# Scatter-adds of one expert declared independent, and the zero fill of the expert rows moved to the kernel's start

## The chip, the cores and the metric

The program runs on one core of a Trainium2 chip. The metric is the device time of one execution in microseconds (us). Before the change it takes 4751.77 us, the median of three runs between 4748.73 and 4754.36 us. All profile times below count from the start of the profiled execution, whose span is 4751.6 us.

A core has five engines that run their own instruction streams in order: PE (TensorE, matrix products and transposes), DVE (VectorE), ACT (ScalarE), POOL (GpSimd) and SP (SyncE, here only a DMA queue). SP and ACT issue the plain transfers; POOL issues the indirect ones (scatters by a list of row numbers) and, in this kernel, the zero fills of large DRAM tables. An instruction that waits for a semaphore holds up everything behind it on its own engine, DMA issues included.

## The reference, cut to what matters

A graph of 3125 nodes with 256 features goes through four blocks, each added to its input:

- three attention layers over 103125 edges (a projection of the nodes, then edge scores, a softmax over the incoming edges and a weighted sum),
- a mixture of 16 experts, of which each node uses its best two,
- a layer that sums neighbours' messages,
- a mixture of 8 experts with one expert per node.

The change is in the second block and in what prepares it. Cut to that:

```python
logits = x @ gate_w + gate_b
top_probs, top_idx = top_k(softmax(logits), 2)
top_probs = top_probs / sum(top_probs)
hidden = silu(x @ w1[e]) * (x @ w2[e])           # for each expert e
out = sum over the two chosen e of weight[e] * (hidden @ w3[e])
```

Every node thus adds two rows, from two different experts, to its sum. Within one expert no node occurs twice.

## The kernel before, in words

**Tiling.** The nodes lie in 25 tiles of 128 rows (NT, NP = 3200 rows in all). The rows of each expert lie in a table in DRAM, `rows0`, with room for 3200 rows per expert, of which the first 512 (CAP0, four tiles of 128) are used. A row has 258 numbers (1032 bytes): 256 features, the node's number, and its weight. Places of an expert that no node takes must hold zero features and a node number that points to a spare row beyond the real nodes; this is why the first 512 rows of each expert are filled with an "empty" row (L579 to L585) before nodes are scattered into them.

**Routing (L593 to L661).** Layer norm, gate scores, softmax, the best two experts and each node's place in their tables are worked out on PE, DVE and ACT. The last result is `to`, the row numbers (L648). Then 50 indirect DMAs on POOL (L659), two for each tile of nodes, write the nodes' rows into `rows0`. They are declared independent of each other, but they come behind the zero fill, as they write the same table.

**Experts (L664 to L706).** A Python loop, unrolled, over the 16 experts. For expert e:

- ACT issues the loads of `w1`, `w2`, `w3` (L671 to L675), SP the load of the expert's rows `xs` (L677). Pools `rw` and `rx` have two buffers for each name, so what expert e+2 loads goes where expert e's was.
- DVE turns the node numbers of the rows into integers, `who` (L679). This name too has two buffers: `who` of expert e+2 overwrites that of expert e, and may do so only when expert e's scatters, which read it, are over.
- PE transposes the rows (L684), ACT copies them out (`xsT`, L685).
- For each of four slices j of the hidden width, PE forms `p1` and `p2` (both `ps_h` in the profile, L692; two PSUM buffers each), ACT applies silu to `p1` (L695), DVE multiplies by `p2` into `hid` (L696).
- For each of the four row tiles q, PE forms `ps_o` (L700), DVE scales it to `y` (L703), and POOL adds it to the nodes' rows of a DRAM table `sums` by an indirect DMA that accumulates (L704).

The four scatter-adds of an expert, and those of successive experts, all write `sums`, and the framework orders writers of one tensor: each waits for the landing of the one before. At the end `sums` is read back into `x` (L708).

In the profile each float32 product shows as two instructions: 32 of `ps_h` (four slices, two products, two halves of the inner dimension, times two) and 32 of `ps_o` for one expert.

**Order of the work.** The order on each engine comes from the framework's scheduler, not from the Python order alone: it lets later work pass when earlier work is not ready. In the trace DVE runs `who` of expert e+1 before `hid` of expert e.

**The start.** `setup` loads x; `routed` (L868) opens a pool `em` for one 5128-byte-per-partition tile and has POOL write it into the table of the last block, `rows1`, in nine DMAs (`empty_rows`, L854, 8 of 5128 KB and one of 641 KB). The pool closes, and `attention_layers` opens its own pools in the freed SBUF space: first `gw`, with, for each layer, `gw0` (2048 bytes per partition, issued by SP, L272), `ga0` (2048, ACT, L274 and L275) and `gb0` (1024, ACT, L277), then the same for the two other layers. A tile in reused space waits until the old tile's readers, here the zero-fill DMAs, have landed. The projection of the first layer follows (L222 on PE, copies L223 on ACT, scores L230 on DVE), then `build_adjacency`: a preparation (L80 to L135), which loads edges on SP and ACT, and a loop over groups of edges with bounds known only at run time (L157). Every turn of that loop ends with a meeting of all five engines.

Of the kernel before, what the change touches and what calls it, by code (L numbers as in the profile page):

```python
# [9 lines left out]
F32 = mybir.dt.float32  # L10
# [4 lines left out]
OP = mybir.AluOpType  # L15
# [4 lines left out]
P = 128  # L20
# [3 lines left out]
NP = NT * P  # L24
D = 256
# [9 lines left out]
NX0, HID0 = 16, 512  # L35
# [482 lines left out]
CAP0 = 512  # L518
CAP1 = 1024
SLOTS = (N + NX1 * (P - 1)) // P  # L520
ROW0 = D + 2
ROW1 = HID1 + D + 2
SPARE = NP


def counters(tc, cp):

    nc = tc.nc
    before = cp.tile([P, P], BF16, name="before")
    nc.gpsimd.memset(before, 1.0)  # L530

    nc.gpsimd.affine_select(before, before, pattern=[[1, P]], compare_op=OP.is_gt, fill=0.0, base=0,
                            channel_multiplier=-1)
    every = cp.tile([P, P], BF16, name="every")
    nc.gpsimd.memset(every, 1.0)
    return before, every


def independent(tc, group, made):

    tc.declare_no_dep(made.ins, group=group, reason="rows of different tokens")
    tc.add_to_no_dep_group(group, made.ins)
# [21 lines left out]
            nc.scalar.copy(xnT[:, :, t * P:(t + 1) * P], ps)  # L564


def routed_experts(tc, x, ident, eps, iota, count, gate_w, gate_b, w1, w2, w3, over):

# [2 lines left out]
    nc = tc.nc  # L573
    before, every = count
    nh = HID0 // P
    with tc.tile_pool(name="rd", bufs=1, space=DRAM) as dp, tc.tile_pool(name="r1", bufs=1) as cp:
        rows = dp.tile([NX0 * NP, ROW0], F32, name="rows0")
        sums = dp.tile([NP + P, D], F32, name="sums0")
        empty = cp.tile([P, ROW0], F32, name="empty")  # L579
        nc.vector.memset(empty, 0.0)  # L580
        nc.gpsimd.iota(empty[:, D:D + 1], pattern=[[0, 1]], base=SPARE, channel_multiplier=1,
                       allow_small_or_imprecise_dtypes=True)
        for e in range(NX0):
            nc.sync.dma_start(rows[e * NP:e * NP + CAP0].rearrange("(q p) f -> p q f", p=P),
                              empty[:, None, :].to_broadcast([P, CAP0 // P, ROW0]))  # L585
        nc.scalar.dma_start(sums[:NP].rearrange("(t p) f -> p t f", p=P), x)
        nc.scalar.dma_start(sums[NP:], empty[:, :D])
        gw = cp.tile([P, KD, NX0], F32, name="gate_w")
        nc.sync.dma_start(gw, gate_w.rearrange("(k p) e -> p k e", p=P))
        gb = cp.tile([P, NX0], F32, name="gate_b")  # L590
# [2 lines left out]
        with tc.tile_pool(name="rgk", bufs=1) as kp, tc.tile_pool(name="rgw", bufs=2) as wp, \  # L593
# [20 lines left out]
            for j, m in enumerate((m1, m2)):  # L614
# [6 lines left out]
                                    channel_multiplier=-1)  # L621
# [6 lines left out]
            for t in range(NT):  # L628
# [10 lines left out]
                           allow_small_or_imprecise_dtypes=True)  # L639
# [3 lines left out]
            for j, hot in enumerate((hot1, hot2)):  # L643
# [7 lines left out]
                           allow_small_or_imprecise_dtypes=True)  # L651
            for t in range(NT):
                n = P if t < NT - 1 else LAST
                for j in range(2):
# [6 lines left out]
                        in_=row[:n], in_offset=None, bounds_check=NX0 * NP - 1, oob_is_err=False))  # L661

        nq = CAP0 // P
        with tc.tile_pool(name="rw", bufs=2) as ep, tc.tile_pool(name="rx", bufs=2) as xp, \  # L664
             tc.tile_pool(name="rs", bufs=3) as sp, \
             tc.tile_pool(name="rpt", bufs=2, space=PSUM) as tp, \
             tc.tile_pool(name="rp1", bufs=2, space=PSUM) as pp, \
             tc.tile_pool(name="rp2", bufs=2, space=PSUM) as po:
            for e in range(NX0):
                a = ep.tile([P, KD, HID0], F32, name="w1")  # L670
                nc.scalar.dma_start(a, w1[e].rearrange("(k p) h -> p k h", p=P))  # L671
                b = ep.tile([P, KD, HID0], F32, name="w2")
                nc.scalar.dma_start(b, w2[e].rearrange("(k p) h -> p k h", p=P))
                o = ep.tile([P, nh, D], F32, name="w3")
                nc.scalar.dma_start(o, w3[e].rearrange("(k p) f -> p k f", p=P))  # L675
                xs = xp.tile([P, nq, ROW0], F32, name="xs")
                nc.sync.dma_start(xs, rows[e * NP:e * NP + CAP0].rearrange("(q p) f -> p q f", p=P))  # L677
                who = xp.tile([P, nq], I32, name="who")
                nc.vector.tensor_copy(who, xs[:, :, D])  # L679
                xsT = xp.tile([P, KD, CAP0], F32, name="xsT")  # L680
                for k in range(KD):
                    ps = tp.tile([P, CAP0], F32, name="ps_x")
                    for q in range(nq):
                        nc.tensor.transpose(ps[:, q * P:(q + 1) * P], xs[:, q, k * P:(k + 1) * P], ident)  # L684
                    nc.scalar.copy(xsT[:, k], ps)  # L685
                hid = xp.tile([P, nh, CAP0], F32, name="hid")
                for j in range(nh):
                    p1 = pp.tile([P, CAP0], F32, name="ps_h1")
                    p2 = pp.tile([P, CAP0], F32, name="ps_h2")
                    for ps, w in ((p1, a), (p2, b)):  # L690
                        for k in range(KD):
                            nc.tensor.matmul(ps, w[:, k, j * P:(j + 1) * P], xsT[:, k], start=(k == 0),  # L692
                                             stop=(k == KD - 1))
                    s = sp.tile([P, CAP0], F32, name="silu")
                    nc.scalar.activation(s, p1, AF.Silu)  # L695
                    nc.vector.tensor_tensor(hid[:, j], s, p2, op=OP.mult)  # L696
                for q in range(nq):
                    ps = po.tile([P, D], F32, name="ps_o")
                    for j in range(nh):
                        nc.tensor.matmul(ps, hid[:, j, q * P:(q + 1) * P], o[:, j], start=(j == 0),  # L700
                                         stop=(j == nh - 1))
                    y = sp.tile([P, D], F32, name="y")
                    nc.vector.tensor_scalar(y, ps, xs[:, q, D + 1:D + 2], None, op0=OP.mult)  # L703
                    nc.gpsimd.indirect_dma_start(  # L704
                        out=sums[:, :], out_offset=bass.IndirectOffsetOnAxis(ap=who[:, q:q + 1], axis=0),
                        in_=y, in_offset=None, bounds_check=NP + P - 1, oob_is_err=True, compute_op=OP.add)  # L706
            for t in range(0, NT, 5):
                nc.sync.dma_start(x[:, t:t + 5], sums[t * P:(t + 5) * P].rearrange("(t p) f -> p t f", p=P))  # L708

# [144 lines left out]
def empty_rows(tc, cp, rows):  # L854

    nc = tc.nc
    empty = cp.tile([P, ROW1], F32, name="empty1")
    nc.vector.memset(empty, 0.0)
    nc.gpsimd.iota(empty[:, HID1 + D:HID1 + D + 1], pattern=[[0, 1]], base=SPARE, channel_multiplier=1,
                   allow_small_or_imprecise_dtypes=True)  # L860
    for e in range(NX1):
        nc.gpsimd.dma_start(rows[e * NP:e * NP + CAP1].rearrange("(q p) f -> p q f", p=P),
                            empty[:, None, :].to_broadcast([P, CAP1 // P, ROW1]))
    nc.gpsimd.dma_start(rows[NX1 * NP:], empty)


@with_exitstack
def routed(ctx: ExitStack, tc: tile.TileContext, i: dict, out: bass.AP, over):  # L868
    nc = tc.nc
    const = ctx.enter_context(tc.tile_pool(name="const", bufs=1))  # L870
    dram = ctx.enter_context(tc.tile_pool(name="dram", bufs=1, space=DRAM))
    x, ident, eps, iota = setup(tc, const, i)
    count = counters(tc, const)
    rows = dram.tile([NX1 * NP + P, ROW1], F32, name="rows1")
    with tc.tile_pool(name="em", bufs=1) as em:
        empty_rows(tc, em, rows)

    ct = [dram.tile([P, NP], F32, name=f"ct{b}") for b in range(NT)]
    neg = [dram.tile([P, NP], BF16, name=f"neg{b}") for b in range(NT)]
    layers = [[i[f"L0_gnn_{n}{j}"] for n in ("W", "al", "ar", "b")] for j in (1, 2, 3)]  # L880
    attention_layers(tc, x, ident, eps, ct, neg, i["src"], i["dst"], layers)

    late = ctx.enter_context(tc.tile_pool(name="late", bufs=1))
    weights = top1_weights(tc, late, *(i["L1_ffn_" + n] for n in ("W1", "b1", "Wg", "bg", "Wd", "bd")), ident)
    routed_experts(tc, x, ident, eps, iota, count,
                   *(i["L0_ffn_" + n] for n in ("gate_w", "gate_b", "w1", "w2", "w3")), over[:, 0:1])
    xnT = late.tile([P, KD, NP], F32, name="xnT")
    layernorm_t(tc, x, xnT, ident, eps)
    sum_layer(tc, x, xnT, ct, i["L1_gnn_W"], i["L1_gnn_M"])
    layernorm_t(tc, x, xnT, ident, eps)  # L890
    routed_top1(tc, x, xnT, ident, iota[:, NX0 - NX1:], count, weights, rows, out, over[:, 1:2])
# [81 lines left out]
```

## Time and profile before

| What | Value |
|---|---|
| Device time | 4751.77 us |
| PE busy | 3457.9 us, 73% of the span |
| DVE busy | 2261.3 us, 48% |
| ACT busy | 769.3 us, 16% |
| POOL busy | 247.0 us, 5% |
| First projection product (L222) | at 122.69 us |
| First group of the edge loop (L161) | at 173.51 us |
| First indirect store of rows (L659) | at 3437.33 us |
| First expert's first product (L692) | at 3514.74 us |
| Last scatter-add landed, x read back from | 4004.88 us |

The span falls into the start and adjacency (to 1961 us), three attention layers (to about 3369 us), routing (to 3507 us), the 16 experts (to 4005 us), the sum layer and the last block. Only the chain view and the waits of one stage tell what that stage is bound by; the shares of the whole span are means over all of them.

### The profile page before, as it was taken

The page shows a single profiled execution, that of the slowest core. Times are in us where ns is not written, and L with a number is a line of the kernel's source. Part 1 is how long each engine was busy: PE and PEld are TensorE (multiplying, and loading weights), DVE is VectorE, ACT ScalarE, POOL GpSimd, SP SyncE. Part 2 cuts the span into 40 slices and gives each one's busy share as a digit, 9 for nine tenths or more (in the row PEclk, how much of TensorE's full clock was granted, in tenths as well). Part 3 has the DMA queues.
Part 4 walks back from the last instruction along what each step waited for, and adds up shares of the span by engine and source line. Part 5 has one row for each costly group of instructions (what it writes and reads, how often), then busy time and mean ns, then how long its engine had stood idle before and what let it go on. Part 6 is the DMA issues. An engine that isn't in the chain of part 4 may idle for free. (4 is left out here: it accounts for less than half of the span.)

```text
span 4751.6 us, 53978 instructions
## 1 busy us (share of the span) xinstructions
PE 3457.9 (73%) x15718; PEld 2262.2 (48%) x15718; DVE 2261.3 (48%) x5414; ACT 769.3 (16%) x822; POOL 247.0 (5%) x258
## 2 busy tenths in 40 slices
PE   0666666666666666588888888888537786998978
PEld 0322222222222222377767776777424443886456
DVE  1555555555555555576756665777411112002322
ACT  0100000000000000133333333333121111001310
POOL 0000000000000000000000000000042211000211
PEclk7788888888888898899999998999768887999989
DMA  9101000010010101233333333433633333331233
GB/s 386 27 35 42 28 35 32 31 42 28 35 42 21 42 28 42 106 137 129 142 118 132 138 132 119 152 145 139 200 114 81 89 88 106 111 139 56 109 121 111
DMA packets 122345, 452.30 MB, mean 95 GB/s; under 512 B 13778, under 2 KB 66834, under 8 KB 106133
## 3 DMA queue, kind: packets, MB, share of 16 engines
q1 hardware_dynamic: 57336, 260.79, 15.4%
q10 hardware_dynamic: 38478, 112.15, 6.8%
q0 software_dynamic: 26320, 76.75, 5.1%
q8 instruction: 106, 1.74, 0.1%
q14 instruction: 105, 0.86, 0.1%
HBM read 299.62 MB, written 151.02 MB: 95 GB/s over the span
## 5 line engine op out<-in xcount | busy, mean ns | idle before, releaser
L171 PE MATMUL acc<-ohk,ohs 125*128 125x512 f16 (+1 forms) x4260 | 1025.0, 393 | 497.1 <-DVE ohs L167 451.2
L339 PE MATMUL acc<-h,pt 128*128 128x257 f32 x3750 | 931.0, 398 | 160.4 <-DVE pt L335 160.3
L171 PEld LDWEIGHTS <-ohs 125*128 125x128 f16 x4260 | 423.0, 111 | 1102.5 <-DVE ohs L167 519.5
L339 PEld LDWEIGHTS acc<-h,pt 128*128 128x128 f32 x3750 | 715.2, 197 | 300.5 <-DVE pt L335 191.6
L169 DVE TENSOR_SCALAR ohk<-iota_k,kw 125x1600 f16<-125x1600 f16 x1065 | 672.1, 631 | 0.0
L335 DVE TENSOR_TENSOR pt<-ps_t,cb 128x512 f32<-128x512 f32 (+1 forms) x525 | 314.1, 626 | 406.2 <-PE ps_t L333 405.1
L167 DVE TENSOR_SCALAR ohs<-iota_s,sw 125x128 f16<-125x128 f16 x1065 | 249.4, 251 | 236.4 <-PE acc L171 234.7
L180 ACT COPY blk<-acc 128x512 f32<-128x512 f32 x98 | 57.4, 586 | 1740.6 <-PE acc L174 1702.1
L692 PE MATMUL ps_h<-xsT,w 128*128 128x512 f32 x512 | 259.9, 667 | 93.8 <-DVE hid L696 90.3
L325 ACT ACTIVATE z<-z,er 128x3200 f32<-128x3200 f32 x75 | 222.2, 2963 | 623.4 <-DVE r L343 589.0
L333 PE MATMUL ps_t<-ident,z 128*128 128x128 f32 x1875 | 243.6, 274 | 55.7 <-ACT z L327 55.7
L443 PE MATMUL ps_s<-msg,s_ct 128*128 128x256 f32 x1250 | 273.9, 379 | 0.0
L319 DVE CUSTOM_DVE_ANT_0 z<-el_row,nb 128x3200 f32<-128x3200 f32 x75 | 261.0, 3482 | 15.6 <-DMA nb<-neg 14.8
L326 DVE SCALAR_TENSOR_TENSOR z<-z 128x3200 f32<-128x3200 f32 x75 | 261.7, 3489 | 7.1 <-ACT z L325 7.0
L333 PEld LDWEIGHTS ps_t<-ident,z 128*128 128x128 f32 x1875 | 220.2, 141 | 79.2 <-ACT z L327 56.3
L443 PEld LDWEIGHTS ps_s<-msg,s_ct 128*128 128x128 f32 x1250 | 237.5, 190 | 32.3
L327 ACT ACTIVATE z<-z,m 128x3200 f32<-128x3200 f32 x75 | 222.4, 2965 | 127.7 <-DVE m L324 78.9
L692 PEld LDWEIGHTS ps_h<-xsT,w 128*128 128x128 f32 x512 | 107.1, 215 | 237.1 <-issue 124.3
L161 DVE SCALAR_TENSOR_TENSOR kw<-win,key 125x5 f32 x213 | 35.2, 165 | 377.0 <-PEq L157 340.0
L444 DVE SCALAR_TENSOR_TENSOR x<-ps_s,x 128x256 f32<-128x256 f32 x25 | 10.6, 425 | 309.2 <-PE ps_s L443 309.2
L843 PE MATMUL ps_y<-t_wd,hsT 128*128 x512 | 120.9, 390 | 8.7 <-ACT hsT L840 8.7
L704 POOL DMA_INDIRECT sums<-y,who x64 | 98.8, 1544 | 401.7 <-DVE y L703 235.8
(239 smaller groups left out, 2411.8 us busy)
## 6 DMA issues: line engine op xcount, KB each, us to landing
cb<-ct SPq DMA_DIRECT2D x75, 1600.0 KB, 6.6
nb<-neg ACTq DMA_DIRECT2D x75, 800.0 KB, 4.5
rows<-empty POOLq DMA_DIRECT2D x8, 5128.0 KB, 65.0
ct<-blk SPq DMA_DIRECT2D x25, 1600.0 KB, 5.2
s_ct<-ct SPq DMA_DIRECT2D x25, 1600.0 KB, 6.5
w<-in_L_ffn_w_dram ACTq DMA_DIRECT2D x48, 512.0 KB, 3.8
hs<-rows SPq DMA_DIRECT2D x32, 641.0 KB, 4.2
neg<-nb ACTq DMA_DIRECT2D x25, 800.0 KB, 3.3
```

The source lines that it names most:

```text
L167: nc.vector.tensor_scalar(ohs, iota_s[:EP], sw[:, g:g + 1], None, op0=OP.is_equal)
L169: nc.vector.tensor_scalar(ohk, iota_k[:EP], kw[:, g:g + 1], None, op0=OP.is_equal)
L171: nc.tensor.matmul(acc[:, c, :n], ohs, ohk[:, c0:c0 + n], start=False, stop=False, skip_group_check=True)
L319: nc.vector.tensor_tensor_reduce(z, el_row, nb, 1.0, -3e38, OP.add, OP.max, m[:, 0:1])
L325: nc.scalar.activation(z, z, AF.Identity, bias=er[:, b:b + 1])
L326: nc.vector.scalar_tensor_tensor(z, z, 0.2, z, op0=OP.mult, op1=OP.max)
L327: nc.scalar.activation(z, z, AF.Exp, bias=m[:, 1:2])
L333: nc.tensor.transpose(ps[:, j], z[:, (s0 + j) * P:(s0 + j + 1) * P], ident)
L335: nc.vector.tensor_tensor(pt[:, :n], ps[:, :n], cb[:, s0 * P:(s0 + n) * P].rearrange("p (s d) -> p s d", d=P), op=OP.mult)
L339: nc.tensor.matmul(acc, pt[:, j], h[:, s0 + j], start=(s0 + j == 0), stop=(s0 + j == NT - 1))
L443: nc.tensor.matmul(ps, cb[:, s], msg[:, s], start=False, stop=(s == NT - 1))
L692: nc.tensor.matmul(ps, w[:, k, j * P:(j + 1) * P], xsT[:, k], start=(k == 0), stop=(k == KD - 1))
```

## The change

One part lets the four scatter-adds of one expert go without waiting for each other: each is put in a group of its expert, within which no order is kept. So that the unused places of different row tiles don't point to the same spare row, the spare rows become 512 (`CAP0`) in place of 128, and each of the 512 empty places of an expert gets its own. The pool of `y` and `silu` gets a fourth buffer.

The other part takes the zero fill of `rows0` out of the routing and puts it at the beginning of `routed`, on POOL's queue ahead of the fill of `rows1`. Its source tile now holds all four row tiles: 4 x 258 numbers, 4128 bytes per partition, first in pool `em`, ahead of the 5128-byte tile of `rows1`. It is for having the table ready before routing needs it.

```diff
-        rows = dp.tile([NX0 * NP, ROW0], F32, name="rows0")
-        sums = dp.tile([NP + P, D], F32, name="sums0")
-        empty = cp.tile([P, ROW0], F32, name="empty")
-        nc.vector.memset(empty, 0.0)
-        nc.gpsimd.iota(empty[:, D:D + 1], pattern=[[0, 1]], base=SPARE, channel_multiplier=1,
-                       allow_small_or_imprecise_dtypes=True)
-        for e in range(NX0):
-            nc.sync.dma_start(rows[e * NP:e * NP + CAP0].rearrange("(q p) f -> p q f", p=P),
-                              empty[:, None, :].to_broadcast([P, CAP0 // P, ROW0]))
+        sums = dp.tile([NP + CAP0, D], F32, name="sums0")
+        spare = cp.tile([P, D], F32, name="spare")
+        nc.vector.memset(spare, 0.0)
         nc.scalar.dma_start(sums[:NP].rearrange("(t p) f -> p t f", p=P), x)
-        nc.scalar.dma_start(sums[NP:], empty[:, :D])
+        for q in range(0, CAP0, P):
+            nc.scalar.dma_start(sums[NP + q:NP + q + P], spare)
...
-             tc.tile_pool(name="rs", bufs=3) as sp, \
+             tc.tile_pool(name="rs", bufs=4) as sp, \
...
-                    nc.gpsimd.indirect_dma_start(
+
+                    independent(tc, f"sums{e}", nc.gpsimd.indirect_dma_start(
                         out=sums[:, :], out_offset=bass.IndirectOffsetOnAxis(ap=who[:, q:q + 1], axis=0),
-                        in_=y, in_offset=None, bounds_check=NP + P - 1, oob_is_err=True, compute_op=OP.add)
+                        in_=y, in_offset=None, bounds_check=NP + CAP0 - 1, oob_is_err=True, compute_op=OP.add))
...
+    rows0 = dram.tile([NX0 * NP, ROW0], F32, name="rows0")
     rows = dram.tile([NX1 * NP + P, ROW1], F32, name="rows1")
     with tc.tile_pool(name="em", bufs=1) as em:
+        empty = em.tile([P, CAP0 // P, ROW0], F32, name="empty")
+        nc.vector.memset(empty, 0.0)
+        nc.gpsimd.iota(empty[:, :, D], pattern=[[P, CAP0 // P]], base=SPARE, channel_multiplier=1,
+                       allow_small_or_imprecise_dtypes=True)
+        for e in range(NX0):
+            nc.gpsimd.dma_start(rows0[e * NP:e * NP + CAP0].rearrange("(q p) f -> p q f", p=P), empty)
         empty_rows(tc, em, rows)
```

More of the change, by code (lines that the diff above doesn't have):

```diff
@@ L564, in layernorm_rows, with routed_experts @@
             nc.scalar.copy(xnT[:, :, t * P:(t + 1) * P], ps)
-def routed_experts(tc, x, ident, eps, iota, count, gate_w, gate_b, w1, w2, w3, over):
+def routed_experts(tc, x, ident, eps, iota, count, rows, gate_w, gate_b, w1, w2, w3, over):
     nc = tc.nc
@@ L884, in routed @@
     weights = top1_weights(tc, late, *(i["L1_ffn_" + n] for n in ("W1", "b1", "Wg", "bg", "Wd", "bd")), ident)
-    routed_experts(tc, x, ident, eps, iota, count,
+    routed_experts(tc, x, ident, eps, iota, count, rows0,
                    *(i["L0_ffn_" + n] for n in ("gate_w", "gate_b", "w1", "w2", "w3")), over[:, 0:1])
```

## The prediction

> **What bounds the kernel now.** I read the chain of work that ended last first. It runs through the expert stage as one string of `sums` landings with stretches marked issue between them, so I took that stage's waits (3510 to 4005 us: name waited for, total us, times, longest).
>
> ```profile
> POOL sums L704 <- DVE y L703: 235.8, 19, 30.5
> DVE who L679 <- DMA sums<-y,who: 210.5, 14, 16.4
> POOL sums L704 <- DMA sums<-y,who: 162.9, 44, 6.5
> PE ps_h L692 <- DVE hid L696: 90.3, 14, 7.8
> ```
>
> The reader is to see a loop: POOL's scatter-adds wait for each other (44 times), DVE's `who` for the last of them (14 times, once per expert from the third on), PE for `hid`, which stands behind `who` on DVE. The timeline of one expert shows the same in order of time:
>
> ```profile
> 3614.30 0.17 DVE L679 CAST who<-xs 128x4 int32<-128x4 f32 x1 [15.61 <-DMA sums<-y,who]
> 3615.14 7.23 PE L692 MATMUL ps_h<-xsT,w 128*128 128x512 f32 x12 [7.01 <-DVE hid L696]
> ...
> 3622.21 7.07 PE L700 MATMUL ps_o<-w,hid 128*128 128x256 f32 x32
> ...
> 3624.90 1.54 POOL L704 DMA_INDIRECT sums<-y,who  x1 [12.94 <-DVE y L703]
> ...
> 3630.39 8.85 PE L692 MATMUL ps_h<-xsT,w 128*128 128x512 f32 x20 [0.24 <-ACT xsT L685]
> ...
> 3640.99 1.54 POOL L704 DMA_INDIRECT sums<-y,who  x1 [2.94 <-DMA sums<-y,who]
> 3644.92 0.17 DVE L679 CAST who<-xs 128x4 int32<-128x4 f32 x1 [15.12 <-DMA sums<-y,who]
> ```
>
> PE runs 20 of the next expert's 32 products, has both `p2` buffers full and stands still for 6.5 to 7 us until the scatters have landed one by one (3624.90 to 3644.7). The stage's opening shows what PE needs without that wait:
>
> ```profile
> 3514.74 14.82 PE L692 MATMUL ps_h<-xsT,w 128*128 128x512 f32 x32
> ...
> 3529.40 7.07 PE L700 MATMUL ps_o<-w,hid 128*128 128x256 f32 x32
> ...
> 3537.58 8.85 PE L692 MATMUL ps_h<-xsT,w 128*128 128x512 f32 x20 [0.24 <-ACT xsT L685]
> ```
>
> For the zero fill, the routing timeline and its table of stretches (stretch, length, PE, PEld, DVE, ACT, POOL busy, PE clock, DMA share, GB/s):
>
> ```profile
> 3422.74 0.16 DVE L648 CAST to<-to_f 128x25 int32<-128x25 f32 x1
> 3437.33 1.06 POOL L659 DMA_INDIRECT rows<-row,to  x1 [67.28 <-issue]
> ```
>
> ```profile
> 3415.00:3420.00 5.00, 0.67 (x3) 0.10 (x1) 3.89 (x24) 0.00 (x0) 0.00 (x0) 0.50 1.10 274
> 3425.00:3430.00 5.00, 0.00 (x0) 0.00 (x0) 0.00 (x0) 0.00 (x0) 0.00 (x0) 0.50 1.09 257
> ```
>
> `to` is ready at 3422.9, yet POOL starts at 3437.3: the fill was still landing, with all DMA engines busy. And the start, where the fill goes now:
>
> ```profile
> 80.00:100.00 20.00, 0.00 (x0) 0.00 (x0) 0.00 (x0) 0.00 (x0) 0.00 (x0) 0.50 1.02 410
> ```
>
> ```profile
> 117.55 1.41 SPq L272 DMA_DIRECT2D gw<-in_L_gnn_W_dram  x3
> ...
> 122.69 7.54 PE L222 MATMUL ps_m<-gw,xnT 128*128 128x256 f32 x24 [70.12 <-DMA gw<-in_L_gnn_W_dram]
> ```
>
> Nothing computes from 53 to 122 us: the weights' SBUF space is free only when the fill of `rows1` has landed (117.5).
>
> **What the Trainium skill says.** DMA: Bandwidth & Descriptors, "Rules for kernel authors": an accumulating DMA beside another access to the same bytes loses updates, so a wait is needed where rows can repeat; within one expert they can't. The same page, "Queues, rings and completion order": descriptors are taken in ring order without a barrier, so stores without waits overlap. The trace agrees for plain scatters: L659 starts every 1.28 us though each lands 2.5 us after issue. No run yet shows it for accumulating ones. TensorE: Matmul & The Clock Gate, Part 1: after some 3.4 us of idleness the array runs at half clock until it has been busy as long. The trace agrees: 12 products after the wait take 7.23 us, against 8.85/20 x 12 = 5.3 us in the run without one. DMA page, "Specifications": 512-byte pieces suffice for line rate. The trace does not agree: the fill in 1032-byte rows moves 257 to 274 GB/s with the engines full, the 5128-byte rows of `rows1` 410.
>
> **The change part by part.**
>
> *Scatters.* From a start of `ps_o` (time 0 below; 3622.21 in the excerpt): the next expert's `ps_h` starts at 8.18 (3630.39; the same from 3529.40 to 3537.58). 32 products at 8.85/20, less its 0.27 of start-up, are 13.7 us, so the next `ps_o` could start at 21.9. What could stop it: PE's 21st product, at 8.18 + 8.85 = 17.0, needs `hid` 0, so `who` must be through by about 16.2. `who` needs two things. (a) The scatters: `y` 0 is ready at 2.4, POOL starts at 2.7; without waits the next follow at 1.54 us each plus the 0.31 us that POOL shows between the stores of L659, so 2.7, 4.5, 6.4, 8.2 (`y` 3 is ready at 7.6). The last lands 3.8 us later by the median, at 12.0; by the slowest seen (7.3) at 15.5. (b) `xs` for two experts on: issued when `y` 3 is done, at 7.6, landing 4.9 to 8.7 us later: 12.6 to 16.3. Both end before 16.2 save at their worst, so PE becomes the bound. I take 22.1 us per expert, 0.2 for odd late landings; bounds 21.9 and 24. Before: `ps_o` of the first expert at 3529.40, of the last 1.93 us ahead of its first `y` (3986.92), 3985.0; 455.6/15 = 30.4 us each. Saved: 455.6 - 15 x 22.1 = **124**. After the last `ps_o` start the end came 19.9 us later (4004.88); it will come at 12.0: **8** more. The extra buffer and the 384 more spare rows (3 issues of 0.48 us on ACT at 3366, where ACT waits anyway) cost nothing; the fourth `y` buffer only keeps `y` from waiting.
>
> *Fill out of routing.* POOL can start 0.3 us after `to`, 3423.1 in place of 3437.3: **14** saved. Nothing else gates it: the big loads ahead on SP were issued by 3400. The 50 stores behind it keep their pace.
>
> *Fill at the start.* 16 x 516 KB = 8.45 MB. At 260 GB/s that is 32.5 us of full DMA engines, at 410 GB/s 20.6; I take the former. So the last zero lands at 117.5 + 32.5 = 150. Who waits for that? Here I must judge the placement. The new 4128-byte tile comes first in its pool. If tiles lie one behind another, `gw0` and `ga0` (2048 + 2048 = 4096 bytes) fall wholly inside it and wait for the small fill alone; `gb0` and layer 2's weights fall on the 5128-byte tile and wait till 150. That a wait follows the place and not the pool, the trace supports: `h`, in the same group of later pools but elsewhere, is set at 2.47 us. The small fill, with x's 3.3 MB beside it, is through at about 3 + 11.7/0.26 = 48 us. And the scheduler lets ready work pass: in the trace ACT does all 25 copies of `xnT` (L215) before it stops at the `ga` issues that stand ahead of them in the program. So I expect ACT to do the 25 `h` copies before `gb0`, and the edge loads to come before it too. Then: weights at about 55, projection 31 us as now (124.9 to 156), preparation 24 us as now (147 to 171) and up to 15 more for loads beside a full DMA: done by about 125, under the fill. The loop's first turn can't end sooner than all engines meet, so not before ACT and SP have issued what stood behind 150. In the profile before, those issues and their landing took from 117.5 to 129.8; seven of the nine are left, about 10 us, and the meeting 2: the second turn starts near 162, against 181.5 (L161). **19.5** saved.
>
> Sum: 124 + 8 + 14 + 19.5 = 165.5; 4751.8 - 165.5 = **4586**.
>
> **The rivals.**
>
> 1. *The start is lost, not won.* If ACT's or SP's stream takes the later weights first, or the tiles lie otherwise, everything from L222 on moves by the fill: +32.5 (20.6 at the fast rate). Time: 4586 + 19.5 + 32.5 = **4638** (4626). For it: all nine `ga`/`gb` issues stand ahead of the first `h` copy now. Against: then they all waited for the same landing.
> 2. *A new wait takes over at `who`.* If accumulating stores slow each other, or `xs` lands at its 8.7 with the weights beside it, the period becomes, say, 26: 15 x 3.9 = 58 more, **4644**. For: the second scatter of an expert, beside the weights, lands after about 6 us already. Against: DMA share is 0.31 to 0.43 in this stage.
> 3. *Slower.* The scatters don't overlap at all (the engines finish one row store before the next), so the period stays 30.4, and the start is lost: 4751.8 + 32.5 - 14 = **4770**. Against it: the pace of L659.
>
> **How the numbers follow.** The forecast 0.68, rival 1 0.18, rival 2 0.10, rival 3 0.04. The range goes from 4568 (fill at 410 GB/s: 12 less; period 21.9: 3 less; shorter loads in routing: 3 less) up to 4645, which takes in rivals 1 and 2. Faster 0.95, same 0.01, slower 0.04.
>
> **What would show it.** Right: the waits of `sums` on `sums` nearly gone, 32 `ps_h` in a row at some 14 us, a `ps_o` every 22 us, first L659 right after L648, L222 near 55 us with DMA still full. Wrong: L222 near 155 (rival 1); `who` still waiting for `sums` or now `xs`, with PE idle behind `hid` (rival 2 or 3). The weakest step is the order on ACT and SP at the start.

## The result and the profile after

The changed kernel takes 4633.0 us (median of 4 runs, 4630.2 to 4638.1) against 4753.1 us (4 runs of the kernel before): a ratio of 0.975, 95% interval 0.9733 to 0.9766. That is 120 us saved. The forecast was 165.5 us saved, 4586; the time lies inside the range given and almost on rival 1 (4638). That it lies inside is luck as far as the forecast's own sum goes: the range reached that far only because it took in rivals 1 and 2. The profile says where the sum went wrong: the expert stage gave what was expected, and the start went the other way.

The waits of the expert stage after the change (3525 to 3886 us: name waited for, total us, times, longest):

```profile
POOL sums L700 <- DVE y L698: 254.1, 16, 30.6
...
DVE who L674 <- DMA sums<-y,who: 97.6, 14, 8.4
```

L700 is the accumulating store, L704 before. Of its 44 waits for itself none is left; POOL waits for `y` once per expert. `who` (L674) still waits for the stores 14 times, but for 7 us in place of 15. Whether that hurts is seen in the order of one expert:

```profile
3551.34 14.00 PE L687 MATMUL ps_h<-xsT,w 128*128 128x512 f32 x32 [0.24 <-ACT xsT L680]
...
3557.98 0.17 DVE L674 CAST who<-xs 128x4 int32<-128x4 f32 x1 [7.23 <-DMA sums<-y,who]
...
3565.18 7.07 PE L695 MATMUL ps_o<-w,hid 128*128 128x256 f32 x32
...
3567.87 1.54 POOL L700 DMA_INDIRECT sums<-y,who  x1 [14.32 <-DVE y L698]
...
3569.71 1.54 POOL L700 DMA_INDIRECT sums<-y,who  x1 [0.30 <-issue]
...
3571.56 1.54 POOL L700 DMA_INDIRECT sums<-y,who  x1 [0.30 <-issue]
```

It doesn't: all 32 `ps_h` products run in one go of 14.00 us, while `who` waits beside them. The stores start 1.85 us apart, and from the start of an expert's first store to the moment `who` goes through it takes 11.6 us (3546.36 to 3557.98), where it took 20.0 before (3624.90 to 3644.92). The Trainium skill's page DMA: Bandwidth & Descriptors, "Queues, rings and completion order", says that data descriptors carry no barrier between them, in a passage on the queues of SP and ACT; the trace now agrees for accumulating stores that POOL issues.

The clock that TensorE was granted, a column of the table of stretches, is 1.00 from 3545 to 3860 us, against a mean of 0.89 before (3530 to 3980). With the wait, the slow products behind it are gone too: of the 8.3 us saved per expert some 6.5 are the wait, and 1.9 are what the 12 products after it lost in the prediction's excerpt (7.23 us against 5.3).

The start is the other half. The first line is the table of stretches from 60 to 80 us (columns as in the prediction), the second fence the timeline:

```profile
60.00:80.00 20.00, 0.00 (x0) 0.00 (x0) 0.00 (x0) 0.00 (x0) 0.00 (x0) 0.50 1.02 410
```

```profile
146.75 1.41 SPq L272 DMA_DIRECT2D gw<-in_L_gnn_W_dram  x3
...
152.54 24.48 PE L222 MATMUL ps_m<-gw,xnT 128*128 128x256 f32 x100 [103.84 <-DMA gw<-in_L_gnn_W_dram]
```

The idle stretch has not been filled with the projection, as forecast; it has grown. All three `gw` loads are issued together at 146.75, 29.2 us later than before (117.55), so the first layer's weights waited for the whole fill. And the routing:

```profile
3444.78 0.16 DVE L643 CAST to<-to_f 128x25 int32<-128x25 f32 x1
3445.68 1.08 POOL L654 DMA_INDIRECT rows<-row,to  x1 [51.52 <-DVE to L643]
```

The first store follows `to` at once. Stage by stage, from the two profiles (4751.6 and 4630.7 us); `kw` is DVE's first instruction in each turn of the edge loop, `gate_w` the load with which the routing begins:

| stretch | before, us | after, us | difference |
|---|---|---|---|
| start to first `kw` (L161) | 173.5 | 202.9 | +29.4 |
| first `kw` to `gate_w` (adjacency, attention) | 3192.1 | 3186.8 | -5.3 |
| `gate_w` to first row store | 71.8 | 56.0 | -15.8 |
| first to last row store | 63.3 | 68.5 | +5.2 |
| last row store to first `ps_o` | 28.8 | 29.0 | +0.2 |
| first to last `ps_o` start | 455.6 | 330.4 | -125.2 |
| last `ps_o` start to the reload of `x` | 19.9 | 12.0 | -7.9 |
| the rest | 746.7 | 745.1 | -1.6 |

### The profile page after: what moved, and what is told of

It is laid out like the page before. It is cut to its first block, busy times and chain, and to the rows that moved or that the text cites. A ratio compares the mean times of both kernels' runs of the same rounds, so it can differ in the third digit from the quotient of the medians.

```text
span 4630.7 us, 53964 instructions
## 1 busy us (share of the span) xinstructions
PE 3415.7 (74%) x15718; PEld 2248.5 (49%) x15718; DVE 2262.6 (49%) x5415; ACT 769.1 (17%) x822; POOL 259.2 (6%) x274
## 5 line engine op out<-in xcount | busy, mean ns | idle before, releaser
L687 PE MATMUL ps_h<-xsT,w 128*128 128x512 f32 x512 | 225.0, 597 | 3.6 <-ACT xsT L680 3.6
L161 DVE SCALAR_TENSOR_TENSOR kw<-win,key 125x5 f32 x213 | 35.3, 166 | 377.2 <-PEq L157 340.4
L687 PEld LDWEIGHTS ps_h<-xsT,w 128*128 128x128 f32 x512 | 96.3, 191 | 122.9 <-issue 110.6
L230 DVE SCALAR_TENSOR_TENSOR junk<-h,ga 128x256 f32<-128x256 f32 x150 | 57.6, 421 | 124.8 <-ACT h L223 123.0
```

## The experiments

Where nothing else is said, an edit is shown against the kernel after, and a ratio is to the kernel before, run beside it.

The theory after the result: the stores' part saves some 133 us (125.2 + 7.9) and the fill's move loses (29.4 - 15.8, some 13.6), because the first layer's weights wait for the fill as a whole, and not for the bytes that they cover. Rivals: the fill's move is neutral or a gain that something else hides; the wait follows something other than pools; the fill's mere length in DMA time is what is lost.

### 1. The fill's move alone

```
-                    independent(tc, f"sums{e}", nc.gpsimd.indirect_dma_start(
+                    nc.gpsimd.indirect_dma_start(
...
-             tc.tile_pool(name="rs", bufs=4) as sp, \
+             tc.tile_pool(name="rs", bufs=3) as sp, \
```

> The kernel after, with the four accumulating stores of an expert waiting for each other again and three y buffers; the zero fill stays at the very beginning. Theory (the move of the fill alone loses, the stores alone win): the start ends 29.3 us later as in the kernel after, routing gives back 15.8, the expert stage is that of before (a ps_o every 30.4 us, 19.9 us from the last ps_o to the end): 4753 + 29.3 - 15.8 = 4766.5, up to 4772 with the slower row stores of L654. Rival (my forecast's start was only hidden by something in the stores): 4753 - 14 - 19.5 = 4719.5. Second rival (the fill's move is neutral within what can be measured): 4753.

Measured: 4769.1 us against 4755.7 of before, ratio 1.003 (1.002 to 1.0039). The move of the fill alone makes the kernel 13 us slower. Its waits in the expert stage (3525 to 4015 us) are those of before:

```profile
POOL sums L700 <- DVE y L698: 236.0, 20, 30.4
DVE who L674 <- DMA sums<-y,who: 211.3, 14, 16.3
POOL sums L700 <- DMA sums<-y,who: 159.6, 43, 6.5
```

So the 120 us saved are some 133 won by one part and 13 lost by the other.

### 2. Only `who` set free, in the kernel before

If PE stood still because `who` has two buffers and blocks `hid` behind it on DVE, more buffers for `who` should do as much as independent stores.

```
-             tc.tile_pool(name="rs", bufs=3) as sp, \
+             tc.tile_pool(name="rs", bufs=3) as sp, tc.tile_pool(name="rh", bufs=4) as wp, \
...
-                who = xp.tile([P, nq], I32, name="who")
+                who = wp.tile([P, nq], I32, name="who")
```

> The kernel before, with who alone in a pool of its own with four buffers; the four accumulating stores still wait for each other and the fill stays in routing. Theory (what held PE was not the row of stores itself but that who, with two buffers, stands on DVE ahead of hid until the stores of two experts back have read it): the row of four serial stores takes some 20 us from the first start to the last landing, less than PE's 22 us per expert, so with who set free PE becomes the bound: period near 22 to 24 us, 15 x 6.4 to 8.4 = 96 to 126 saved, 4627 to 4657. xs keeps two buffers, is read by the last y and so lands up to 16 us into the period, just in time. Rival (the serial stores are the bound by themselves, each expert's row of stores being nearer 27 to 30 us with its wait for y and its turns): no change, 4740 to 4753.

Measured: 4627.4 us, ratio 0.9732 (0.9719 to 0.9745). This one buffer count saves as much as the whole change, with every store still held in order behind the one ahead. Its waits (3510 to 4005 us), then its timeline:

```profile
DVE who L679 <- DMA xs<-rows: 90.3, 16, 15.4
POOL sums L704 <- DMA sums<-y,who: 89.0, 28, 6.0
```

```profile
3600.26 1.54 POOL L704 DMA_INDIRECT sums<-y,who  x1 [3.96 <-DVE y L703]
...
3604.70 1.54 POOL L704 DMA_INDIRECT sums<-y,who  x1 [2.90 <-DMA sums<-y,who]
...
3605.75 14.00 PE L692 MATMUL ps_h<-xsT,w 128*128 128x512 f32 x32 [0.24 <-ACT xsT L685]
...
3611.97 1.54 POOL L704 DMA_INDIRECT sums<-y,who  x1 [5.73 <-DVE hid L696]
...
3616.53 1.54 POOL L704 DMA_INDIRECT sums<-y,who  x1 [3.02 <-DMA sums<-y,who]
...
3619.59 7.07 PE L700 MATMUL ps_o<-w,hid 128*128 128x256 f32 x32
```

The four stores still take 16.3 us from the first start (3600.26) to the last (3616.53), but PE runs 14.00 us through beside them. `who` no longer waits for `sums` at all, only for its own data. From 3597.57 to 3619.59 is 22.02 us per expert, as in the kernel after. The serial stores were never longer than PE's own work; it was the one tile that they kept from being written again, by an engine (DVE) on which `hid`, PE's next input, was queued behind that write.

### 3. Serial stores and a free `who`, in the kernel after

The same edit as in 2, on the kernel of 1 (fill at the start, stores serial).

> The kernel after with the four stores of an expert waiting for each other again, and who in a pool of its own with four buffers. Theory (either way of freeing who gives PE its 22.0 us per expert; the stores' independence beyond that shortens only the tail, 13.4 us from the last ps_o product to the end where they are serial, 5.4 where not): 4633 + 8 = 4641, between 4637 and 4646. Rival (both parts are needed where xs and the stores come late): 4650 to 4700. Second rival (independence brings nothing at all once who is free): 4633.

Measured: 4640.4 us (4635.9 to 4642.6), ratio 0.9765 (0.9751 to 0.9778), against 4633.0 of the kernel after. The 7 us between them are not clear of noise: two kernels of experiment 4 that start no sooner than the kernel after, and do the same work, read 4640.4 and 4638.3. The profile says more. Its waits (3525 to 4015 us):

```profile
POOL sums L700 <- DMA sums<-y,who: 103.1, 27, 6.7
...
DVE who L674 <- DMA xs<-rows: 75.7, 15, 5.6
```

A `ps_o` comes every 22.0 us here too, and from the last `ps_o` start to the reload of `x` it takes 19.9 us against 12.0. So once `who` is free, independence is worth the 8 us of the tail, and nothing in each expert.

### 4. Whose wait is it at the start: four combinations of pools

The forecast took `gw0` and `ga0`, 4096 bytes that lie inside the small fill tile's 4128, to wait for that tile alone. Both fills shared one pool, and all nine weights of the three layers another. First the fill's pool was parted:

```
-    with tc.tile_pool(name="em", bufs=1) as em:
-        empty = em.tile([P, CAP0 // P, ROW0], F32, name="empty")
+    with tc.tile_pool(name="em0", bufs=1) as em0, tc.tile_pool(name="em", bufs=1) as em:
+        empty = em0.tile([P, CAP0 // P, ROW0], F32, name="empty")
```

> The kernel after, with the small fill's tile in a pool of its own around that of the rows1 fill; the tiles keep their places in SBUF. Theory (later tiles wait for all that used a closed pool, not for the bytes that they cover): gw of layer 1 and its ga now wait for the small fill alone, so L222 starts near 50 to 60 us in place of 152.5, and the second turn of the loop is gated by the landing of the large fill and what stands behind it: 160 or so in place of 211, so 4633 - 49 = 4584, between 4575 and 4600. Rival (the wait is for every transfer ahead whatever the pools are, or ACT's and SP's streams take the later weights first): L222 stays near 150, 4633.

Measured: 4640.4 us (4635.2 to 4643.7), with the projection (L222) no sooner than in the kernel after:

```profile
152.33 23.21 PE L222 MATMUL ps_m<-gw,xnT 128*128 128x256 f32 x100 [103.34 <-DMA gw<-in_L_gnn_W_dram]
```

The theory as I had put it, that the old pool is what counts, fell. Then the weights' pool was parted as well:

```
-    with tc.tile_pool(name="gw", bufs=1) as cp, tc.tile_pool(name="gh", bufs=2) as hp:
+    with tc.tile_pool(name="gw0", bufs=1) as c0, tc.tile_pool(name="gw", bufs=1) as cp, \
+         tc.tile_pool(name="gh", bufs=2) as hp:
...
-            wt = cp.tile([P, KD, D], F32, name=f"gw{i}")
+            wt = (cp if i else c0).tile([P, KD, D], F32, name=f"gw{i}")
...
-            at = cp.tile([P, 2, D], F32, name=f"ga{i}")
+            at = (cp if i else c0).tile([P, 2, D], F32, name=f"ga{i}")
```

> The kernel of the two pools for the fill (small tile in its own pool), and on the other side the first layer's gw and ga, 4096 bytes, in a pool of their own that lies inside the small tile's 4128 bytes; the other weights in the pool after it. Theory (a new pool waits for every closed pool that its whole extent touches, so one pool for all nine weights waited for both fills): now gw and ga of layer 1 wait for the small fill alone, as my forecast had it: L222 near 50 to 60 us, the fill and the later weights' issues done near 160, the loop's second turn there in place of 211: 4640 - 50 = 4590, between 4575 and 4605. Rival (the wait is for all fill transfers whatever the pools): L222 near 150, 4640. Second rival (the first layer starts early, but the end of the loop's first turn comes no sooner, since what stood behind the fill moves as a block): L222 near 55 and 4620 to 4640.

Measured: 4571.5 us (4566.9 to 4582.8), ratio 0.9624 (0.9609 to 0.964). All tiles lie at the same SBUF addresses as in the kernel after and the instructions do the same work; only the pools that the tiles belong to differ. Its start, on SP's queue, PE and DVE:

```profile
42.15 0.39 SPq L273 DMA_DIRECT2D gw<-in_L_gnn_W_dram  x1
...
151.51 0.89 SPq L273 DMA_DIRECT2D gw<-in_L_gnn_W_dram  x2
```

```profile
50.78 23.24 PE L222 MATMUL ps_m<-gw,xnT 128*128 128x256 f32 x100 [4.00 <-DMA gw<-in_L_gnn_W_dram]
```

```profile
125.57 0.17 DVE L161 SCALAR_TENSOR_TENSOR kw<-win,key 125x5 f32 x1 [2.25 <-issue]
...
163.59 0.17 DVE L161 SCALAR_TENSOR_TENSOR kw<-win,key 125x5 f32 x1 [31.94 <-PEq L157]
```

The first layer's `gw` goes at 42, the other two at 151.5 when the fill is through. This is the start of the forecast (weights at about 55, preparation done at about 125, second turn near 162): 50.8, 125.6 and 163.6. The fourth combination parts the weights' pool alone, with the edits of the last diff on the kernel after:

> The kernel after, with one pool for both fills as there, but gw and ga of the first layer in a pool of their own inside the small tile's bytes: the fourth of the four combinations. Theory (both sides count as wholes: a new pool waits for the last transfer of every closed pool that it touches): the first layer waits for both fills, L222 near 150 us, 4633. Rival (the old tile counts by its own bytes and only the new pool as a whole): L222 near 51, as with both pools split, 4572.

Measured: 4638.3 us (4633.6 to 4640.2), and the projection late again:

```profile
151.68 24.35 PE L222 MATMUL ps_m<-gw,xnT 128*128 128x256 f32 x100 [102.32 <-DMA gw<-in_L_gnn_W_dram]
```

Parting only one of the two changes nothing. So in these four both sides count as wholes: a tile of a new pool waits for the last transfer out of every closed pool that any part of the new pool lies on.

### 5. A fill whose space no one asks for

```
-    with tc.tile_pool(name="gw", bufs=1) as cp, tc.tile_pool(name="gh", bufs=2) as hp:
+    with tc.tile_pool(name="gw", bufs=1) as cp, tc.tile_pool(name="gh", bufs=2) as hp, \
+         tc.tile_pool(name="em", bufs=1) as em:
...
         h, el, er = fresh()
+        if fill is not None:
+            fill(em)
```

> The kernel after, with both fill tiles in a pool that stays open until attention is done, so that no later tile takes their place; the fill is issued right after the first weights' loads. Theory (the start is lost only to the wait of the weights for the fill's SBUF): no wait of gw or ga for the fill; L222 starts at 25 to 55 us, beside the fill; the first turn of the loop then ends when the fill has landed, near 146, and the second starts near 150 in place of 211: 4633 - 61 = 4572, between 4560 and 4590. Rival (the fill itself, 29 us more of full DMA, is what is lost, wherever its tile lies): the first turn ends no sooner than in the kernel after less the projection's 30 us at most, 4600 to 4633.

Measured: 4577.4 us (4572.2 to 4585.1), ratio 0.962 (0.9604 to 0.9636). The call of the fill has become a function that is handed the pool. No weight waits for the fill, and the start still falls short of what was expected:

```profile
142.62 0.17 DVE L161 SCALAR_TENSOR_TENSOR kw<-win,key 125x5 f32 x1 [2.47 <-issue]
...
160.21 0.17 DVE L161 SCALAR_TENSOR_TENSOR kw<-win,key 125x5 f32 x1 [12.13 <-PEq L157]
```

`L222` started at 65, not at 25 to 55: `x` and the weights now share full DMA engines with the fill (a share of 1.03 to 1.04 from 20 to 60 us). Without a fill at the start, in the kernel of experiment 6, the same products start at 29. The second turn comes at 160.2, ten later than expected, close to experiment 4's 163.6.

The next kernel puts the call of the fill behind `build_adjacency` in the program, in the same kept pool:

```
         build_adjacency(tc, src, dst, ident, ct, neg)
+        if fill is not None:
+            fill(em)
```

> The kernel after, with both fill tiles in a pool that stays open until attention is done, and the whole fill issued only when the adjacency is built. Theory (the fill costs nothing where no one needs its SBUF and the DMA engines have room): nothing waits at the start; L222 starts at 25 to 35 us, once x has landed, and the loop starts 50 us later as in the kernels before and after, near 80 in place of 203: 4633 - 123 = 4510, between 4500 and 4525. Rival (the fill collides with attention's loads, about 120 us of full DMA engines): it gives back 20 to 120 us there, 4530 to 4630.

Measured: 4591.0 us (4585.4 to 4600.4), slower than with the call at the start, and neither theory's picture. POOL's fills:

```profile
3.72 6.20 POOL L881 DMA_DIRECT2D rows<-empty  x8
...
93.85 0.92 POOL L861 DMA_DIRECT2D rows<-empty  x1
373.10 0.88 POOL L861 DMA_DIRECT2D rows<-empty  x1 [278.33 <-SPq L153]
...
```

The place in the program didn't hold the fill back. It has nothing to wait for, so the scheduler let it pass to the very start, the rest into the loop's turns. The second turn started at 135.15, not 88, and from there to the last `kw` (1943.8) took 1809 us against 1769 in the kernel after: 39 given back.

### 6. A fill that can't pass ahead

Here the pool of the fill (the same function as in 5) is opened only once the adjacency's pools are closed, so that the fill has to wait for their space:

```
-        with tc.tile_pool(name="gr", bufs=1) as rp, tc.tile_pool(name="gb", bufs=2) as bp, \
+        with tc.tile_pool(name="em", bufs=1) as em, tc.tile_pool(name="gr", bufs=1) as rp, tc.tile_pool(name="gb", bufs=2) as bp, \
...
+            if fill is not None:
+                fill(em)
```

> The kernel after, with the pool of both fill tiles opened only when the adjacency's pools are closed and kept open through attention: the tiles can't be set before, so no fill can pass ahead to the start. Theory (what the kernel that kept the fill's pool still lost at the start was the fill ahead of x's load and of the first turns, passed ahead because it was ready): L222 at 20 to 35 us, loop start 50 us later, second turn near 85 in place of 211, so 126 less than 4633; the fill's some 120 us of full DMA engines fall into attention, whose loads keep the engines 0.35 to 0.45 busy and are asked for ahead, and cost 0 to 30 us there: 4507 to 4537. Rival (the fill there delays attention's loads by its own length, since they share the engines): 4600 to 4630, no better than the kernel that kept the pool (4577 to 4591).

Measured: 4495.4 us (4494.1 to 4499.5), ratio 0.9462 (0.9448 to 0.9477): 257 us less than before, 138 less than the change. The first `kw` comes at 81.99 us and the fill runs beside attention, from 1854 us on. Its table of stretches (stretch, length, PE, PEld, DVE, ACT, POOL busy, PE clock, DMA share, GB/s):

```profile
1880.00:1920.00 40.00, 27.88 (x141) 23.83 (x142) 27.59 (x40) 16.79 (x9) 9.49 (x12) 0.80 1.02 351
1920.00:1960.00 40.00, 37.17 (x191) 31.49 (x189) 27.51 (x44) 13.16 (x8) 0.56 (x1) 0.96 1.02 417
1960.00:2000.00 40.00, 32.82 (x164) 27.76 (x165) 27.96 (x48) 14.22 (x9) 0.00 (x0) 0.96 1.02 418
...
2080.00:2120.00 40.00, 35.00 (x181) 29.62 (x180) 27.50 (x50) 16.12 (x9) 0.00 (x0) 0.96 0.34 124
```

The first line is where the fill costs something: PE works 27.9 us, and 37.4 in the kernel after at the same distance from the last `kw` (2023 to 2063 us). After that, with the DMA engines still full, it works as much (37.2 and 32.8 of 40 us) as when the fill is over (35.0). From the last `kw` to `gate_w` took 1416.6 us against 1409.1: 7.5 us is the price of the whole fill there. Of the 138 us won over the kernel after, 120.9 are the start (first `kw` 202.92 to 81.99). Another 22.2 lie in the adjacency (first to last `kw` 1777.7 to 1755.5), which I had not expected.

### 7. Longer pieces

```
-            nc.gpsimd.dma_start(rows0[e * NP:e * NP + CAP0].rearrange("(q p) f -> p q f", p=P), empty)
+            nc.gpsimd.dma_start(rows0[e * NP:e * NP + CAP0].rearrange("(p q) f -> p q f", p=P), empty)
```

> The kernel after, with the fill of rows0 written in pieces of 4128 bytes in place of 1032 (each partition fills four rows that lie together; the spare places stay distinct within an expert). Theory (the length of a piece sets the rate: 1032-byte rows 257 to 300 GB/s, 4128 and more 410): 8.45 MB take 20.6 us in place of 29, so gw is issued near 138 in place of 146.75, and all after it 8 to 9 us sooner: 4624 to 4626. Rival (the low rate at the start is that of x's load and of the issues on POOL, not of the pieces): 146.75 again, 4633.

Measured: 4621.6 us (4620.1 to 4628.0), ratio 0.9727 (0.9714 to 0.9741), 11 less than the kernel after. In the profiles 8.5 of them lie at the start (first `kw` at 194.41 in place of 202.92); more than the rest is the row stores, which took 63.3 us here in place of 68.5 (see the fill out of routing, below). The stretch from 20 to 40 us, first in the kernel after, then with long pieces, and then SP's queue:

```profile
20.00:40.00 20.00, 1.43 (x7) 1.34 (x8) 4.42 (x17) 1.00 (x3) 7.77 (x11) 1.00 1.03 287
```

```profile
20.00:40.00 20.00, 6.98 (x37) 4.65 (x38) 10.02 (x32) 6.18 (x18) 8.87 (x11) 1.00 1.03 411
```

```profile
138.77 1.41 SPq L272 DMA_DIRECT2D gw<-in_L_gnn_W_dram  x3
```

The engines are full in both, but 1032-byte rows move 287 GB/s and 4128-byte pieces 411. The Trainium skill's DMA: Bandwidth & Descriptors, "Specifications", gives 512 bytes as enough for line rate; here they weren't, and the measurement decides. `gw` goes 8.0 us sooner. With the length, the number of pieces and where each begins changed too; which of these sets the rate was not parted.

The same edit in the kernel of 6:

> The kernel with the fill in attention, and the fill of rows0 in pieces of 4128 bytes in place of 1032. Theory (the fill is hidden there): within 5 us of that kernel. Rival (the fill's length in full DMA engines is what attention loses): 9 to 12 us less than it.

Measured: 4497.9 us (4496.3 to 4499.5) against 4495.4: no difference. Once it is hidden, the fill's length costs nothing.

## Why the prediction was right or wrong, point by point

**What bounds the kernel: right, and closer to the cause than its own remedy.** It named three waits: stores for stores, `who` for the stores, PE for `hid` behind `who`. Experiment 2 shows that cutting the middle one alone gives all of PE's gain.

**Scatters: right in mechanism and in size.** Forecast 22.1 us per expert and 124 saved; measured 22.03 and 125.2. Forecast end 12.0 us after the last `ps_o` start, 8 saved; measured 12.05 and 7.9. The pitch of 1.85 us was the one worked out. One term was too small: the last store was to land 12.0 us after the start of `ps_o`, but in the four experts from 3543 to 3624 us `who` went through after 14.3 to 14.8, with the last store landing 6.0 to 6.6 us after its start, against 3.9 in series. PE needed it by 16.2, so the forecast held with some 1.5 us to spare. Whether the stores slow each other or the weights' loads beside them do was not parted; the longer period of rival 2 and rival 3 (no overlap) are out.

**Fill out of routing: right.** Forecast 14, measured 15.8. (Before, it was SP that issued this fill, not POOL.) The 50 stores behind it took 5.2 us longer than before, where the prediction had them keep their pace; but experiment 2, which leaves the fill in routing, takes 68.5 us for them as well (3434.0 to 3502.5), and experiments 3 and 7 with the fill at the start take 63.3. Of the thirteen profiles seven have 63.2 or 63.3 and six 68.2 to 69.0; in those six a store waits 1.8 us or more for the landing of another, in the seven at most 0.3. So that isn't the change's doing, and what decides it is open.

**Fill at the start, its length: a term a little too large.** 32.5 us at 260 GB/s were forecast; 29.2 were measured, which is 8.45 MB at 289 GB/s. Experiment 7 shows that the same bytes in longer pieces go faster.

**Fill at the start, who waits: wrong. This is the step that failed.** "A wait follows the place and not the pool" was judged from `h`, which is set at 2.47 us. But `h` lies on no closed pool at all: the nine weights in front of it take 3 x 5120 = 15,360 bytes, and the two fill tiles together 9256. So it couldn't tell the two apart. The nine weights of one pool lie on two tiles of another, and each side counted as a whole. With both parted, the start runs as forecast (experiment 4). The step's cost: second turn at 211.3 where 162 was forecast, 49 us; the total missed by 47. In the prediction this was the step marked weakest, but the weakness was named as the order on ACT and SP, and that order was not at fault: with both pools parted it came out as forecast.

**Rival 1 gave the right time, by a neighbouring cause.** It had +32.5 "if ACT's or SP's stream takes the later weights first, or the tiles lie otherwise". Neither: the tiles lay as assumed. Its chance of 0.18 was too low, since the forecast's own case rested on one indirect sign.

**Left open.** From first `kw` to `gate_w` the kernel after takes 5.3 us less than before, with the same instructions. All of it lies in the adjacency (1783.0 to 1777.7); two other kernels with the fill at the start take 1782.9 and 1782.8 there (experiment 1 and the first of 4), so it isn't the change's doing. In the kernel of 6 the adjacency takes 22 us less, with the same number of products (5179), which keep PE busy for 1106 us in place of 1134. The granted clock goes along with it: summed from the clock records of the traces, TensorE was granted half its clock for 447 of the 1747 us from the second turn on, against 509 of 1769 in the kernel after (means 0.872 and 0.856), and busy time times clock is nearly equal (964 and 971 us). What makes the clock differ I haven't found. In experiment 4 with both pools parted, and in the first kernel of 5, the second turn of the loop waits till the fill is over; whether for the transfers themselves or for what stands behind them in the queues was not parted.

## What to carry to other kernels

Before breaking a chain of waits, ask which tile the chain keeps, which engine has to write it again, and what is queued there behind that write: here four buffers for a tile of 2 KB did what independent stores did, but for 8 us at the end. A load that is moved "off the path" still waits for, and is waited for by, whatever shares its SBUF: give a long transfer's tile a pool on which no early tile will lie, and hold it back by the space it needs, since a place in the program doesn't hold it. Then look for the stage whose DMA engines have room: the 51 MB of zeroes (16 x 516, 8 x 5128 and 641 KB) cost 7.5 us beside attention, and the start without them is 121 us shorter.

## What the runs showed that was not expected

- The tiles here that take a closed pool's space wait for whole pools on both sides: `L222` at 152.5, 152.3, 151.7 us with none or one of the two pools parted, at 50.8 with both.
- Accumulating stores to different rows overlap when nothing makes them wait: 1.85 us apart, against 4.5 to 7.1 us in series (the expert from 3624.90 us on, in the kernel before).
- DMA engines that are full need not slow the work beside them: attention beside the fill at 417 GB/s lost 7.5 us in 1409, where the fill began.
- Full engines don't mean full rate: at a share of 1.03 both, with the last of x's load beside them, 1032-byte rows moved 287 GB/s and 4128-byte pieces 411.
